# Gathers that add to turned products: an accumulating DMA, and clips on ScalarE, in a graph layer

## Chip, core and metric

One core of a Trainium2 chip runs the whole kernel. The metric is device time in microseconds: 4238.63 us, the median of three runs (4232.95 to 4239.72). All times of the profile are from one further execution of 4239.95 us, whose span (first to last instruction) is 4238.2 us.

## What is computed

A layer of a graph network on 12500 nodes with 96 features and 412500 edges, sorted by the target node. Cut to what matters:

```
_mlp(h, W, b, gamma, beta): h = relu(h @ W + b); normalize h over all rows (mean, variance); gamma * h + beta
node_feat = _mlp(x, W_node, ...)
edge_feat = _mlp(edge_attr, W_edge, ...)
message   = concatenate([x[row], x[col], edge_feat])      # row = src, col = dst
message   = _mlp(message, W_msg, ...)
agg       = segment_sum(message, col)
out       = layernorm(x + agg + node_feat)
```

So each edge's message is relu of a sum of three products: P[src], a row of the table P = x W_msg[0:96] of its source node; Q[dst], a row of the table Q of its target; and a product of the edge's own features.

## The kernel before

Edges stand in tiles of 128; four tiles make a group (512 edges, `GT` = 4, `GE` = 512), four groups a block (`BG` = 4). There are 3223 tiles, 806 groups and 202 blocks. A block's target nodes lie in a narrow window, so Q[dst] needs no gather: a matmul adds it from a window of Q's rows. P[src] does need one: `gather` (L205) issues, on POOL's queue, one indirect DMA per tile, which fetches 128 rows of 384 bytes into a tile `pg`. An index is given per partition.

The program has an opening and a loop. In the opening the tables P and Q are made and stored (`tables`), the edges' features are split and stacked (`split`, `places`), the node part is done (`nodes`) and the statistics of the edge features are taken (`edge_norm`), which the loop's weights `w_e` and `bias` need. POOL gathers meanwhile, in `blocks` (L220): rows of the first `SPILL` = 29 blocks go through a ring of `RING` = 14 groups (seven buffers of two) and are stored by SP to `spill` in HBM, two blocks behind (`BEHIND`). For the first `RAW` = 4 blocks the rows are those of x, since P is not there yet. Three tiles (`EARLY`) are fetched by SP in another way. At the end of the opening the same ring takes the rows of 14 groups more (L519).

`plan` makes the loop's order of blocks: the spilled ("early") ones are strewn among the other 173 ("late") ones. For a block at place s in that order the work is:

- SP: `load(s)` brings the edges' stacked features and the window of Q into `rhs`, three places ahead; `fetch` brings an early block's rows back into `pb`.
- PE and ScalarE: `edges` multiplies, `prepare` (L617) clips into `left`, two places ahead.
- PE and DVE: `linear` (L623) makes one group's product z, features by edges, in PSUM; `by_edge` (L632) turns it by three 32x32-wise transpositions into `zs`, edges by features, in SBUF. One place ahead, two buffers in the free end of `big`. One group's transpositions fill 32 partitions of all 16 tiles of the block.
- DVE: `message` (L639) takes two groups at once: h = clip(z + rows) by one custom instruction (`TENSOR_ADD_SAT`, L649), or a plain clip for raw blocks.
- ScalarE squares h (L663), DVE adds the squares up in PSUM (L674) and makes the matrix of places `at` (L655); PE adds h up by place (`sums`, L693), two groups behind; DVE adds the window to `agg` (L713).
- POOL: `ahead_of` (L489) gathers one group more for each late group taken in, 14 groups ahead.

The order on all engines in the loop is the one in which the program is written; each engine works its queue in order. A gather also waits for the gather eight before it, since eight semaphores go round.

## Time and profile before

| what | value |
|---|---|
| median of the runs | 4238.63 us |
| profiled execution, its span | 4239.95 us, 4238.2 us |
| gathers (from x, from P) | 64, 3156 |
| clipped adds on DVE with gathered rows, with spilled rows | 346, 50 |
| plain clips on DVE (raw blocks) | 8 |
| ScalarE, busy from 710 to 4176 us | 711.8 us |
| TensorE, busy from 710 to 4176 us, granted clock there | 2092.1 us, 0.79 |

The profile page gives, per engine, the time in which it was busy; a group of instructions has its count, its busy time and mean, and the idle time of the engine just before its instructions, with what ended it. "issue" is idle time in which nothing that the profile shows was waited for. PE is the matmul engine, PEld its weight loads, DVE the vector engine, ACT the scalar engine (ScalarE), POOL the engine that issues the gathers, SP the one that issues most other DMAs. A share of busy time over the whole span mixes opening, loop and tail; the views by window keep them apart.

### The profile page before, as it was taken

Reading aid. Unit: us, or ns where it says so; the run is one execution under the profiler, and the core shown is the slowest. Engines: PE = TensorE matmul, PEld = TensorE weight load, DVE = VectorE, ACT = ScalarE, POOL = GpSimd, SP = SyncE. Lnnn points to the kernel's source line nnn. Section 1 sums busy time; section 2 is a strip of 40 time slices with the busy share of each in tenths; the row PEclk is TensorE's granted clock in tenths of the full one; section 3 lists DMA queues with packets and bytes.
Section 4 is the critical chain, followed back from the end, with each engine's and each line's share of the span. In section 5 each row is a group of like instructions: output and inputs, shape, how many; then the busy total and the mean of one; then the engine's idle time right before and its main releaser. Section 6 shows DMA issues by size and latency. Waiting matters only on the chain.

```text
span 4238.2 us, 34504 instructions
## 1 busy us (share of the span) xinstructions
PE 2500.7 (59%) x10245; PEld 1391.0 (33%) x10245; DVE 3340.1 (79%) x4652; ACT 1117.9 (26%) x1229; POOL 3180.5 (75%) x3248
## 2 busy tenths in 40 slices
PE   4156664776655655666655565555655556666556
PEld 3041111433333332333333333333333333333335
DVE  2469998998887877878878887787878877878775
ACT  1438882222221211212112211111112112211111
POOL 7777776777777777777777777777777777777775
PEclk7557776888877787877777877787788787777776
DMA  8746562222222223222222222222222222222222
GB/s 229 267 139 149 134 148 51 57 57 64 50 56 53 57 71 78 63 56 56 55 56 50 57 54 55 57 57 54 56 57 53 50 63 50 54 57 55 56 44 64
DMA packets 215122, 316.63 MB, mean 75 GB/s; under 512 B 126785, under 2 KB 133275, under 8 KB 212095
## 3 DMA queue, kind: packets, MB, share of 16 engines
q0 software_dynamic: 103040, 158.48, 17.6%
q1 hardware_dynamic: 98923, 150.92, 12.1%
q10 hardware_dynamic: 12960, 4.93, 0.5%
q8 instruction: 82, 1.34, 0.1%
q14 instruction: 117, 0.96, 0.1%
HBM read 258.19 MB, written 55.89 MB: 74 GB/s over the span
## 4 chain that ended last, share of the span: by engine, by line
POOL 37%; DVE 25%; issue 19%; DMA 12%; PE 6%; ACT 1%; SPq 0%; DVEq 0%; POOLq 0%; ACTq 0%
POOL pg L210 37%; DMA pg<-p_tab,src 9%; DVE big L636 9%; DVE estats L419 8%; DVE h L649 3%; DVE mixed L674 2%; PE z L626 1%; PE pa L693 1%; PE py L981 1%; DVE at L655 1%; DMA q_tab<-trow 1%; PE py L383 1%; PE pt L194 0%; DMA x<-in_ea 0%; DVE part L424 0%
## 5 line engine op out<-in xcount | busy, mean ns | idle before, releaser
L210 POOL DMA_INDIRECT pg<-p_tab,src x3156 | 3097.6, 981 | 995.2 <-issue 899.6
L636 DVE STREAM_TRANSPOSE big<-z 32x512 f32<-32x512 f32 x2424 | 1715.3, 708 | 90.8 <-PE z L626 29.6
L693 PE MATMUL pa<-at,h 128*97 128x80 f32 x6446 | 934.1, 304 | 1346.3 <-DVE h L649 1327.5
L693 PEld LDWEIGHTS pa<-at,h 128*97 128x97 f32 x6446 | 881.7, 217 | 1818.7 <-DVE h L649 1677.1
L626 PE MATMUL z<-left,rhs 128*96 128x512 f32 (+1 forms) x1616 | 1079.7, 757 | 2.1 <-DVE big L636 2.1
L663 ACT ACTIVATE sq<-h 128x768 f32<-128x768 f32 x403 | 339.5, 842 | 2750.2 <-DVE h L649 2710.1
L649 DVE CUSTOM_DVE_ANT_0 h<-big,pg 128x768 f32<-128x768 f32 x346 | 325.3, 940 | 585.1 <-DMA pg<-p_tab,src 583.0
L621 ACT ACTIVATE left<-pr 127x1024 f32<-127x1024 f32 x404 | 405.6, 1004 | 18.1 <-PE pr L614 18.1
L674 DVE TENSOR_TENSOR mixed<-mixed,sq 128x768 f32<-128x768 f32 x401 | 387.7, 967 | 12.5
L419 DVE BATCH_NORM_STATS2 estats<-r 128x6 f32<-128x512 f32 x606 | 359.7, 682 | 11.8 <-ACT r L417 11.8
L417 ACT ACTIVATE r<-pr 128x1024 f32<-128x1024 f32 x303 | 309.0, 1025 | 102.2 <-PE pr L413 54.4
L413 PE MATMUL pr<-ea,wide 128*128 128x512 bf16 x606 | 237.8, 486 | 126.8 <-ACT r L417 116.7
L655 DVE TENSOR_TENSOR at<-rel,mixed 128x1264 f32<-128x1264 bf16 x202 | 296.5, 1468 | 6.8
L614 PE MATMUL pr<-late,we 128*128 128x512 bf16 x692 | 287.1, 507 | 23.4 <-DMA rhs<-q_tab 12.2
L626 PEld LDWEIGHTS z<-left,rhs 128*96 128x96 f32 x1616 | 264.1, 212 | 8.0 <-DVE big L636 6.5
L614 PEld LDWEIGHTS <-we 128*128 128x128 bf16 x808 | 103.3, 128 | 448.2 <-issue 446.5
L413 PEld LDWEIGHTS <-wide 128*128 128x128 bf16 x606 | 66.6, 110 | 297.4 <-issue 277.9
L383 PE MATMUL py<-center,big 96*128 96x96 f32 x196 | 42.8, 423 | 113.2 <-ACT big L378 100.2
L383 PEld LDWEIGHTS py<-center,big 96*128 96x128 f32 x196 | 42.0, 332 | 114.0 <-ACT big L378 100.6
L210 POOL DMA_INDIRECT pg<-in_x,src_raw x64 | 61.0, 952 | 20.9 <-issue 19.2
L194 PE MATMUL pt<-w_msg,big 96*128 96x192 f32 x196 | 37.8, 360 | 19.6 <-ACT trow L198 13.4
L200 DVE COPY trow<-pt 128x768 f32<-128x768 f32 x14 | 13.1, 956 | 44.5 <-DMA p_tab<-trow 20.7
(128 smaller groups left out, 696.6 us busy)
## 6 DMA issues: line engine op xcount, KB each, us to landing
pg<-p_tab,src POOLq DMA_INDIRECT x3156
pb<-spill SPq DMA_DIRECT2D x29, 768.0 KB
spill<-pg SPq DMA_DIRECT2D x55, 384.0 KB
ea<-stack_d SPq DMA_DIRECT2D x25, 480.0 KB
stack_d<-y SPq DMA_DIRECT2D x24, 448.0 KB
late<-stack_d SPq DMA_DIRECT2D x57, 180.0 KB
rhs<-q_tab SPq DMA_DIRECT2D x202, 46.5 KB
x<-in_ea SPq DMA_DIRECT2D x8, 896.0 KB
```

The source lines that it names most:

```text
L210: made = [nc.gpsimd.indirect_dma_start(out=pg[:, i, :], out_offset=None, in_=tab[:, :], in_offset=bass.IndirectOffsetOnAxis(ap=idx[:, i:i ...
L417: nc.scalar.activation(r, pr, AF.Relu)
L419: nc.vector.bn_stats(stats[:, (k - o) % NS, (k - o) // NS, :], r[:, 1 - o, :])
L614: nc.tensor.matmul(prs[s, half][:, i, :n], we[:, 2 * half + i, :], block[s][:, :n], start=True, stop=True)
L621: nc.scalar.activation(x[:C + WN, 2 * half:2 * half + 2, :n], pr[:C + WN, :, :n], AF.Relu)
L626: nc.tensor.matmul(zt[i % ZB][:C, :n], rhs[:KR, s % RB, i, :], left[s % 2][:KR, i, :n], start=True, stop=not raw)
L636: nc.vector.transpose(zs[s % 2][i * QE:(i + 1) * QE, :n // QE, q * QE:(q + 1) * QE], zt[i % ZB][q * QE:(q + 1) * QE, :n].rearrange("p (t e ...
L649: nc.vector._custom_dve(TENSOR_ADD_SAT, out=h, in0=z, in1=rows, s0=MOST, s1=0.0)
L655: nc.vector.tensor_tensor(at[s % AB][:, :m, :NW - 1], rel.rearrange("p g t -> p (g t)")[:, order[s] * BT:order[s] * BT + m].unsqueeze(2) . ...
L663: nc.scalar.activation(sq[:, :m, :n, :], hb[k // 2 % HP][:, k % 2:k % 2 + m, :n, :C], AF.Square)
L674: nc.vector.tensor_tensor(wide_sq, wide_sq, sq, op=OP.add)
L693: nc.tensor.matmul(by_place[s % 2][:C + 1, :NW], hb[k // 2 % HP][:r, k % 2, t, :], at[s % AB][:r, i * GT + t, :], start=i == 0 and t == 0, ...
```

## The change

- A late block's gathers no longer fill a buffer of their own. They are accumulating DMAs (`compute_op=OP.add`) whose target is the block's turned product in `zs`: each gathered row is added to the 96 numbers that stand there. So they come after the block's transpositions.
- `message` of late and raw blocks is then a clip at zero, on ScalarE (`AF.Relu`). Spilled blocks that aren't raw keep the clipped add on DVE.
- `zs` has six buffers, one block each: the four of the ring that the opening's plain gathers use, now whole blocks (16 groups instead of 14), and two in `big`.
- The loop turns block s+4 (`TURN`) while it takes in block s, and issues the gathers of block s+3 (`AFTER`); four blocks are turned ahead of the loop. Loads, `edges` and `prepare` are moved to as many places earlier (s+6, s+5).
- 32 blocks are spilled, 170 are late. `ahead_of` and the gathers at the opening's end are gone.

```diff
-SPILL = 29 * BG
-RING = 14
+SPILL = 32 * BG
+RING, MORE = 4, 2
+AFTER, TURN = 3, 4
...
-    ring = rpool.enter_context(tc.tile_pool(name="ring", bufs=RING // 2))
+    ring = rpool.enter_context(tc.tile_pool(name="ring", bufs=1))
+    ring = [ring.tile([P, BG, GT, C], F32, name=f"pg{i}") for i in range(RING)]
...
-    def gather(g, pg, without=0):
+    def gather(g, pg, without=0, plus=False):
...
-            in_offset=bass.IndirectOffsetOnAxis(ap=idx[:, i:i + 1], axis=0)).ins
+            in_offset=bass.IndirectOffsetOnAxis(ap=idx[:, i:i + 1], axis=0),
+            **(dict(compute_op=OP.add) if plus else {})).ins
...
-            for g in range(SPILL, SPILL + RING):
-                ahead_of(g)
...
-            zs = [big[:, NN - (i + 1) * BT * C:NN - i * BT * C].rearrange("p (t c) -> p t c", c=C) for i in range(2)]
+            zs = ring + [big[:, NN - (i + 1) * BT * C:NN - i * BT * C].rearrange("p (g t c) -> p g t c", t=GT, c=C)
+                         for i in range(MORE)]
...
-                if order[s] < RAW:
-                    nc.vector.tensor_scalar(h, z, 0.0, MOST, op0=OP.max, op1=OP.min)
-                    return
-                rows = got[g // 2 * 2].rearrange("p m t c -> p (m t) c")[:, o:o + n, :]
-                nc.vector._custom_dve(TENSOR_ADD_SAT, out=h, in0=z, in1=rows, s0=MOST, s1=0.0)
+                if RAW <= order[s] < SPILL // BG:
+                    rows = got[g // 2 * 2].rearrange("p m t c -> p (m t) c")[:, o:o + n, :]
+                    nc.vector._custom_dve(TENSOR_ADD_SAT, out=h, in0=z, in1=rows, s0=MOST, s1=0.0)
+                else:
+                    nc.scalar.activation(h, z, AF.Relu)
...
+                def turned(s, i):
+
+                    if s < len(order):
+                        linear(s, i)
+                        by_edge(s, i)
+
+                def rows_to(s, u):
+
+                    if s < len(order) and order[s] >= SPILL // BG and order[s] * BG + u < NG:
+                        gather(order[s] * BG + u, zs[s % len(zs)][:, u, :, :], plus=True)
...
+                for s in range(TURN):
+                    for i in range(BG):
+                        turned(s, i)
+                    if s < AFTER:
+                        for i in range(BG):
+                            rows_to(s, i)
...
-                    if s + 1 < len(order):
-                        linear(s + 1, u)
-                        by_edge(s + 1, u)
+                    turned(s + TURN, u)
+                    rows_to(s + AFTER, u)
...
-                    if g >= SPILL and ahead < SPILL + len(steps):
-                        ahead_of(ahead)
-                        ahead += 1
```

How this moves instructions is seen in the built programs' order. First POOL, from its first gather on: before (L210), all gathers but those of the raw blocks in two runs, with the load of `flag` between them, and then the sums of squares at the end.

```order
L210 DMA pg<-in_x,src_raw 128x96 x64
L210 DMA pg<-p_tab,src 128x96 x453
L719 TENSOR_LOAD flag
L210 DMA pg<-p_tab,src 128x96 x2703
L682 TENSOR_TENSOR sq<-sq 128x384
```

After (L212), around the load of `flag`; `pg_77` to `pg_80` are the four buffers of the ring, each holding a block of 16 tiles, and `big` stands for the two more.

```order
L212 DMA pg_79<-p_tab,src 128x96 x16
L212 DMA pg_80<-p_tab,src 128x96 x16
L715 TENSOR_LOAD flag
L212 DMA pg_77<-p_tab,src 128x96 x16
L212 DMA pg_78<-p_tab,src 128x96 x16
L212 DMA pg_79<-p_tab,src 128x96 x16
L212 DMA pg_80<-p_tab,src 128x96 x16
L212 DMA big<-p_tab,src 128x96 x32
```

Ahead of `flag` there are 509 gathers instead of 517, and behind it 2711 instead of 2703; those behind it write into buffers that DVE writes first.

Second DVE, at the loop's start: before, the last transpositions (L636) of block 0, with block 1's behind them and the first clipped adds (L649, shown as ISA) between; `z` are the two buffers in PSUM.

```order
L636 STREAM_TRANSPOSE big<-z_4966 32x16x32 x3
L636 STREAM_TRANSPOSE big<-z_4965 32x16x32 x3
L649 ISA h_4955<-big,pg 128x8x96
L636 STREAM_TRANSPOSE big<-z_4966 32x16x32 x3
L636 STREAM_TRANSPOSE big<-z_4965 32x16x32 x3
L649 ISA h_4956<-big,pg 128x8x96
L636 STREAM_TRANSPOSE big<-z_4966 32x16x32 x3
L674 TENSOR_TENSOR mixed<-mixed,sq 128x768
L655 TENSOR_TENSOR at_4962<-rel,mixed 128x16x79
```

After, from the end of the fourth block (its buffer is `pg_80`) on: the transpositions are L632, the squares' sum L670.

```order
L632 STREAM_TRANSPOSE pg_80<-z_4903 32x16x32 x3
L632 STREAM_TRANSPOSE big<-z_4902 32x16x32 x3
L632 STREAM_TRANSPOSE big<-z_4903 32x16x32 x3
L632 STREAM_TRANSPOSE big<-z_4902 32x16x32 x3
L632 STREAM_TRANSPOSE big<-z_4903 32x16x32 x3
L670 TENSOR_TENSOR mixed<-mixed,sq 128x768
L651 TENSOR_TENSOR at_4899<-rel,mixed 128x16x79
L632 STREAM_TRANSPOSE big<-z_4902 32x16x32 x3
```

Four blocks are turned ahead of the loop and a fifth in its first step, and no clipped add stands among them; the clips are on ScalarE, each just ahead of its square.

Third SP, whose queue opens the loop: before, the last stores of spilled rows (L237), the first loads of features (`late`), twelve rows of `bias` (L538) that complete `rhs`, and the windows of Q (L578).

```order
L237 DMA spill<-pg 128x768 x4
L719 TENSOR_LOAD flag
L360 DMA late_4967<-stack_d 32x1536
L360 DMA late_4967<-stack_d 16x1536
L538 DMA rhs<-bias 1x16x6 x12
L360 DMA late_4967<-stack_d 60x1536
```

After, the same place (L240, L533):

```order
L240 DMA spill<-pg_79 128x768 x2
L240 DMA spill<-pg_80 128x768
L715 TENSOR_LOAD flag
L363 DMA late_4904<-stack_d 32x1536
L363 DMA late_4904<-stack_d 16x1536
L533 DMA rhs<-bias 1x16x6
L240 DMA spill<-pg_80 128x768
L533 DMA rhs<-bias 1x16x6 x11
```

The last store, of the second half of block 31, which waits for the last plain gathers, now stands behind the first of the bias rows.

More of the change, by code (lines that the diff above doesn't have):

```diff
@@ L225, in blocks @@
                 for i in range(0, BG, 2):
-                    pg = ring.tile([P, 2, GT, C], F32, name="pg")
+                    pg = ring[b % RING][:, i:i + 2, :, :]
                     for k in range(2):
@@ L487, in fast @@
         y0s, got = [], {}
-        def ahead_of(g):
-            if g % 2 == 0:
-                got[g] = ring.tile([P, 2, GT, C], F32, name="pg")
-            if g < NG:
-                gather(g, got[g // 2 * 2][:, g % 2, :, :])
         with tc.manual_schedule(engines={ET.SP, ET.Pool}):
@@ L632, in by_edge @@
             def by_edge(s, i):
-                n = columns(s)
+                n, z = columns(s), zs[s % len(zs)].rearrange("p g t c -> p (g t) c")
                 for q in range(C // QE):
-                    nc.vector.transpose(zs[s % 2][i * QE:(i + 1) * QE, :n // QE, q * QE:(q + 1) * QE],
+                    nc.vector.transpose(z[i * QE:(i + 1) * QE, :n // QE, q * QE:(q + 1) * QE],
                                         zt[i % ZB][q * QE:(q + 1) * QE, :n].rearrange("p (t e) -> p t e", e=QE))
@@ L642, in message @@
                 o = k % 2 * GT
-                z = zs[s % 2][:, g % BG * GT:g % BG * GT + n, :]
+                z = zs[s % len(zs)].rearrange("p g t c -> p (g t) c")[:, g % BG * GT:g % BG * GT + n, :]
                 h = hb[k // 2 % HP].rearrange("p m t c -> p (m t) c")[:, o:o + n, :C]
-                if order[s] < RAW:
-                    nc.vector.tensor_scalar(h, z, 0.0, MOST, op0=OP.max, op1=OP.min)
-                    return
-                rows = got[g // 2 * 2].rearrange("p m t c -> p (m t) c")[:, o:o + n, :]
-                nc.vector._custom_dve(TENSOR_ADD_SAT, out=h, in0=z, in1=rows, s0=MOST, s1=0.0)
+                if RAW <= order[s] < SPILL // BG:
[3 more added lines that the diff above has]
+                    nc.scalar.activation(h, z, AF.Relu)
             def places_of(s):
@@ L715, in fast, with first @@
             loads = list(range(-(-NB // NBY)))
-            n, ahead = len(steps), SPILL + RING
+            n = len(steps)
             with tc.manual_schedule(engines={ET.SP, ET.Pool, ET.PE, ET.DVE, ET.Activation}):
                 bad = nc.values_load(flag, min_val=0, max_val=1, skip_runtime_bounds_check_because="a comparison's result")
+                def turned(s, i):
[5 more added lines that the diff above has]
+                        gather(order[s] * BG + u, zs[s % len(zs)][:, u, :, :], plus=True)
+                def first(s, half):
+                    if s < len(order):
+                        edges(s, half)
+                        prepare(s, half)
                 for s in range(3):
@@ L723, in fast @@
                     for half in range(2):
-                        edges(s, half)
-                        prepare(s, half)
+                        first(s, half)
                 places_of(0)
-                for i in range(BG):
-                    linear(0, i)
-                    by_edge(0, i)
+                for s in range(TURN):
[4 more added lines that the diff above has]
+                            rows_to(s, i)
+                    if s + 3 < TURN + 2:
+                        load(s + 3)
+                    if s + 2 < TURN + 1:
+                        for half in range(2):
+                            first(s + 2, half)
+                assert min(order.index(b) for b in range(RAW)) >= TURN + 2
                 waiting, last = None, BG * (len(order) - 1)
@@ L734, in fast @@
                     if u == 0:
-                        if s + 3 < len(order):
-                            load(s + 3)
-                        if s + 2 < len(order):
-                            fetch(s + 2)
+                        if s + TURN + 2 < len(order):
+                            load(s + TURN + 2)
+                        for o in (TURN + 2, 2):
+                            if s + o < len(order) and (order[s + o] < RAW) == (o > 2):
+                                fetch(s + o)
                     if k >= LATER:
@@ L755, in fast @@
                         add(j // BG, place(j // BG))
-                    if s + 2 < len(order):
+                    o = s + TURN + 1
+                    if o < len(order):
                         if u % 2 == 0:
-                            edges(s + 2, u // 2)
+                            edges(o, u // 2)
                         else:
-                            prepare(s + 2, u // 2)
-                        if u == 3 and order[s + 2] < RAW:
-                            transposed(s + 2)
-                    if g >= SPILL and ahead < SPILL + len(steps):
-                        ahead_of(ahead)
-                        ahead += 1
+                            prepare(o, u // 2)
+                        if u == 3 and order[o] < RAW:
+                            transposed(o)
                     if k >= 200 and k % 4 == 0 and loads:
```

## Prediction

> **What bounds the kernel now.** I read the page's busy times first, then the groups of POOL, then who waits for whom. The first rows are the page's busy line and its groups that matter here (line, engine, operation, shapes, count, busy time, mean of one in ns, then the idle time before them).

> ```profile
> span 4238.2 us, 34504 instructions
> ...
> PE 2500.7 (59%) x10245; PEld 1391.0 (33%) x10245; DVE 3340.1 (79%) x4652; ACT 1117.9 (26%) x1229; POOL 3180.5 (75%) x3248
> ...
> L210 POOL DMA_INDIRECT pg<-p_tab,src x3156 | 3097.6, 981 | 995.2 <-issue 899.6
> L636 DVE STREAM_TRANSPOSE big<-z 32x512 f32<-32x512 f32 x2424 | 1715.3, 708 | 90.8 <-PE z L626 29.6
> ...
> L649 DVE CUSTOM_DVE_ANT_0 h<-big,pg 128x768 f32<-128x768 f32 x346 | 325.3, 940 | 585.1 <-DMA pg<-p_tab,src 583.0
> ...
> L210 POOL DMA_INDIRECT pg<-in_x,src_raw x64 | 61.0, 952 | 20.9 <-issue 19.2
> ```

> DVE has the longest busy time, but it is not the bound: it idles 583.0 us because gathered rows have not landed. POOL's gathers take 3097.6 us and their "issue" gaps 899.6 us more, together nearly the whole span of 4238.2 us. The waits of POOL from 640 us on say the same (waiter, what it waited for, total, times, longest):

> ```profile
> POOL pg L210 <- issue: 780.0, 2558, 0.3
> POOL pg L210 <- DMA pg<-p_tab,src: 41.2, 135, 0.3
> POOL pg L210 <- DVE h L649: 18.1, 1, 18.1
> POOL pg L210 <- DVE big L636: 7.9, 26, 0.3
> ```

> Apart from one stop of 18.1 us, no gap is longer than 0.3 us, which is what every gather has before it. So the end is set by **when POOL may start its last run of gathers, how many there are, and what each one takes**. The rest is the tail behind the last one.

> What one takes is not constant. Grouped over 400 to 600 us (before the loop) and over 760 to 4100 us (in the loop):

> ```profile
> L210 POOL DMA_INDIRECT pg<-p_tab,src x158 | 149.4, 946 | 51.2 <-issue 45.7 <-DMA spill<-pg 4.5 <-DMA erow<-p_tab 0.9
> ...
> L210 POOL DMA_INDIRECT pg<-p_tab,src x2605 | 2546.0, 977 | 794.3 <-issue 740.0 <-DMA pg<-p_tab,src 39.3 <-DVE big L636 7.6
> ...
> L649 DVE CUSTOM_DVE_ANT_0 h<-big,pg 128x768 f32<-128x768 f32 x329 | 310.2, 943 | 558.7 <-DMA pg<-p_tab,src 556.7
> ...
> L649 DVE CUSTOM_DVE_ANT_0 h<-big,pb 128x768 f32<-128x768 f32 x50 | 46.5, 931 | 0.3
> ```

> In the loop a gather means 977 ns and 305 ns of gap (794.3 / 2605); before the loop 946 ns. The 31 ns more are 2605 x 0.031 = 80.8 us. The timeline shows where they fall:

> ```profile
> 1515.28 0.95 POOL L210 DMA_INDIRECT pg<-p_tab,src  x1 [0.30 <-issue]
> 1516.53 1.25 POOL L210 DMA_INDIRECT pg<-p_tab,src  x1 [0.30 <-DMA pg<-p_tab,src]
> 1518.08 0.94 POOL L210 DMA_INDIRECT pg<-p_tab,src  x1 [0.30 <-issue]
> ...
> 1516.05 0.91 DVE L649 CUSTOM_DVE_ANT_0 h<-big,pg 128x768 f32<-128x768 f32 x1
> ```

> The long gather, 1.25 us, begins while DVE's clipped add is running, and its neighbours beside transposes take 0.94 to 0.95. I charge the 80.8 us to the 379 clipped adds of that window (329 and 50): **0.213 us each**. An undisturbed gather then has a slot of 0.946 + 0.305 = **1.251 us**.

> [...]

> **The change part by part.** Here are the loop's opening and end in the timeline:

> ```profile
> 691.44 0.94 POOL L210 DMA_INDIRECT pg<-p_tab,src  x1 [0.30 <-issue]
> 710.50 0.95 POOL L210 DMA_INDIRECT pg<-p_tab,src  x1 [18.12 <-DVE h L649]
> ...
> 698.48 10.90 DVE L636 STREAM_TRANSPOSE big<-z 32x512 f32<-32x512 f32 x15 [9.30 <-PE z L626]
> ...
> 632.13 2.56 SPq L237 DMA_DIRECT2D spill<-pg  x4
> 678.21 7.56 SPq L538 DMA_DIRECT2D rhs<-bias  x12
> ...
> 4175.19 0.95 POOL L210 DMA_INDIRECT pg<-p_tab,src  x1 [0.30 <-issue]
> ```

> The busy times by window (PE, PEld, DVE, ACT, POOL, each with its count; granted clock, DMA share, GB/s) count POOL's run:

> ```profile
> 710.00:4176.00 3466.00, 2092.13 (x8948) 1185.02 (x8948) 2781.70 (x3815) 711.80 (x811) 2641.66 (x2703) 0.79 0.24 56
> ```

> *Counts.* 3220 gathers before and after (3156 + 64). Before, 2703 are behind the stop and 517 ahead of it. After, the plain ones are 32 x 16 - 3 = 509, and 2711 accumulate: eight more behind the stop, 8 x 1.251 = **+10.0 us**.

> *The start.* A transposition writes 32 partitions of all 16 tiles of a block, a gather adds to 128 partitions of one tile: the first accumulating gather needs all twelve transpositions of its block. At 10.90 / 15 = 0.727 us each, from 698.48, they end at 707.2. I add the usual 0.3 us gap and 0.6 us, since on SP's queue one store of spilled rows (2.56 / 4) now stands among the bias rows that everything here waits for: **708.1 us**, 2.4 us ahead of the 710.50 of now, which waited for a first clipped add to free a buffer. That store waits for the last plain gather, number 509; now that one starts at 691.44 - 8 x 1.25 = 681.4, so at worst SP stands still about 5 us there. The ring of plain gathers is 16 groups instead of 14, which lets POOL run ahead by a half block (10 us) more and so, I take it, not be late. Bounds of the start: 707.5 to 713.

> *The rate.* 396 clipped adds (346 + 50) become 56, two for each of 28 spilled blocks. 340 x 0.213 = **-72.4 us**. ScalarE takes the rest:

> ```profile
> L663 ACT ACTIVATE sq<-h 128x768 f32<-128x768 f32 x403 | 339.5, 842 | 2750.2 <-DVE h L649 2710.1
> ...
> L674 DVE TENSOR_TENSOR mixed<-mixed,sq 128x768 f32<-128x768 f32 x401 | 387.7, 967 | 12.5
> ...
> L655 DVE TENSOR_TENSOR at<-rel,mixed 128x1264 f32<-128x1264 bf16 x202 | 296.5, 1468 | 6.8
> ```

> A clip of this size is not in the trace on ScalarE; by the square of the same size, 842 ns, 348 clips are 293 us on an engine that waits 2710.1 us for exactly these messages. They are hidden, and DVE loses 340 x 0.94 us of work, which is worth nothing since DVE was waiting. Behind a clip that waits for rows stand on ScalarE the square and the next `left`; `left` is made five blocks ahead, so nobody waits for it soon. The three more spilled blocks (six stores, three loads) ride on SP beside POOL's run.

> *The new wait.* Each block's first gather waits for DVE. The loop turns block s+4 while it takes in block s, so when POOL is at the block that is being taken in, three whole blocks, at least two of them with gathers to do, are turned: 2 x 16 x 1.251 = 40 us of cover. DVE's own work for a block is 12 x 0.708 of transposing, 2 x 0.967 of squares and 1.468 of places, 11.9 us and some small adds, against 20 us of POOL. I cost this wait at nothing; if the cover were gone, each microsecond per block would cost 170 us.

> *The gather itself.* The trace holds no accumulating gather. [...] I take **946 ns**, the row it is nearest to: the same 128 rows, the same indices, the same bytes out of the table. [...]

> *The sum.* 708.1 + 2711 x 1.251 + 56 x 0.213 = 708.1 + 3391.5 + 11.9 = 4111.5 us for the end of the last slot. The same sum for the kernel now, 710.5 + 2703 x 1.251 + 396 x 0.213, gives 4176.3; the trace has 4175.19 + 1.25 = 4176.4. The tail is 4238.2 - 4176.4 = 61.8 us, and I add 1 us for the clip and for a landing that adds: span 4174.3. The profiled execution lasted 1.75 us more than its span (4239.95), so 4176 against 4239.95; the runs shown have a median 1.3 us lower (4238.63), hence **4175 us**, 1.5% less.

> **The rivals.**

> *B, the other side: POOL works longer on a gather that adds.* Place: each of the 2711 gathers. [...] Price: 27.1 us for every 10 ns; it decides from (4238.6 - 4175) / 2711 = 23.5 ns, only 2.5% of 946. At half as much again (473 ns) the time is 4175 + 1282 = 5457, at double 6740.

> [...]

> *C: the 16 DMA engines become the bound.*

> ```profile
> q0 software_dynamic: 103040, 158.48, 17.6%
> ```

> 17.6% of 16 engines over 4238.2 us, by 3220 gathers, is 0.23 us on each engine for its eight rows. The limit is the slot of 1.251 us, or 156 ns per row. Plain rows leave a factor of 5.4; if each adding row took what eight take now, 0.23 us, a gather would hold an engine 1.85 us, and POOL, which waits for the gather eight before, would go at that rate: 4175 + 2711 x 0.60 = 5800. Against it: twice the bytes alone are 0.46 us.

> *D: the long gathers stay long,* because something else than the clipped add stretches them (rows landing, for instance, which is when a clipped add starts). Then 72.4 us are not saved: 4247, no change.

> **How the numbers follow.** A, the forecast: 0.52, with a range of its own from 4150 to 4225 (the slot to 5 ns, 14 us; start, tail and remaining adds to 10 us; upward also a gather up to 15 ns dearer). B: 0.27. C: 0.12. D: 0.09. A measurement tells about 0.2%, or 8.5 us, from no change. Faster: A and a bit of C or D below 4230, 0.53; same: D, 0.08; slower: B and C, 0.39. A alone is 0.52, so the range must reach into B: up to 5460 it takes in A, D and B to half as much again; left out are B's far part (0.10), most of C (0.08) and 0.01 below. So 4150 to 5460.

> **What would show it.** Right: the group of gathers in the loop near 950 ns with gaps of 0.305; POOL's waits without an entry for DVE or DMA above 0.3 us, save one stop that ends near 708; 56 clipped adds; the last gather near 4110. B shows in the mean of that group, C in long waits of POOL for its own earlier gathers and a share of their queue many times 17.6%, D in a mean still near 977. If turned blocks come too late, POOL's waits name DVE's transposition with gaps far over 0.3 us. I am wrong above all if an adding gather costs POOL 24 ns more than a plain one.

## The result and the profile after

| | before | after |
|---|---|---|
| median of the runs | 4238.47 us | 5847.15 us |
| lowest to highest, 4 runs each | 4232.95 to 4239.72 | 5846.11 to 5847.83 |
| ratio after to before, 95% interval | | 1.3799 [1.3775, 1.3823] |
| span of the profiled execution | 4238.2 us | 5844.3 us |

The forecast was 4175 us, its range 4150 to 5460. The kernel is 38% slower, above the range.

The first rows are the page of the changed kernel: engines, the queue of the gathers, the share of each engine in the chain that ended last, and its groups of gathers and of clips.

```profile
span 5844.3 us, 34880 instructions
...
PE 2657.9 (45%) x10099; PEld 1521.5 (26%) x10245; DVE 3038.1 (52%) x4304; ACT 1410.5 (24%) x1577; POOL 4783.6 (82%) x3248
...
q0 software_dynamic: 406672, 158.48, 24.9%
...
POOL 71%; issue 16%; DVE 7%; DMA 3%; PE 2%; ACT 1%; SPq 0%; another core or an unknown queue 0%; POOLq 0%; ACTq 0%; DVEq 0%
...
L645 ACT ACTIVATE h<-pg 128x768 f32<-128x768 f32 x216 | 181.2, 839 | 2153.2 <-DMA pg<-p_tab,src 2153.0
...
L645 ACT ACTIVATE h<-big 128x768 f32<-128x768 f32 x132 | 111.2, 842 | 1592.2 <-DMA big<-p_tab,src 1592.2
```

POOL went from 3180.5 to 4783.6 us of work, 1603 us more, and the span grew by 1606 us. The other engines wait for it: ScalarE's clips, the new consumers, stand 2153.0 + 1592.2 us for rows. Bytes of the gathers' queue are the same 158.48 MB as before. The groups of POOL from 1000 to 5500 us, where every gather adds, show where the work is:

```profile
L212 POOL DMA_INDIRECT pg<-p_tab,src x1440 | 2280.6, 1584 | 438.6 <-issue 436.5 <-DMA pg<-p_tab,src 1.2 <-DVE at L651 0.3
L212 POOL DMA_INDIRECT big<-p_tab,src x961 | 1489.8, 1550 | 292.7 <-issue 291.4 <-DMA big<-p_tab,src 1.2
```

Two of the six blocks in the ring (`big`) show the undisturbed value, **1550 ns** against 946 before; the gap is still 0.305 us (292.7 / 961). The other four (`pg`) have 34 ns more on the mean. The timeline shows the first gather that adds, and two that meet a clipped add of a spilled block:

```profile
704.08 1.59 POOL L212 DMA_INDIRECT pg<-p_tab,src  x1 [36.16 <-DVE pg L632]
...
1483.19 2.59 POOL L212 DMA_INDIRECT pg<-p_tab,src  x1 [0.30 <-issue]
1483.45 0.90 DVE L643 CUSTOM_DVE_ANT_0 h<-pg,pb 128x768 f32<-128x768 f32 x1
...
1486.09 1.55 POOL L212 DMA_INDIRECT pg<-p_tab,src  x1 [0.30 <-issue]
...
1489.74 0.96 DVE L643 CUSTOM_DVE_ANT_0 h<-pg,pb 128x768 f32<-128x768 f32 x1
1489.80 2.32 POOL L212 DMA_INDIRECT pg<-p_tab,src  x1 [0.30 <-issue]
```

The loop's run starts at 704.1 us. A clipped add stretches a gather by 1.04 and 0.77 us here. Over all 56 adds the gathers that overlap one took 50.1 us more than 1.550 each, **0.89 us per add**, and the other 2655 show no excess (0.3 ns in the mean). Rebuilt from these terms, 704.1 + 2711 x (1.550 + 0.305) + 50.1 = 5783 us; the last gather ends at 5782.4, and 61.9 us of tail follow.

How far a clipped add stretches a gather can be read off these rows. The gather takes its 1.55 us and, on top, the time from its own start to the add's end, less 0.12 us. The add at 1489.74 ends 0.90 us behind the gather's start, and the gather takes 1.55 + 0.90 - 0.12 = 2.33 us (2.32 in its row); the other ends 1.16 us behind it, and 1.55 + 1.16 - 0.12 = 2.59. So the price of an add isn't a constant: it depends on where in a gather the add falls.

In three of the five series of runs behind this one the kernel before itself took 5540 to 5551 us instead of 4237 to 4243, for a reason that the traces don't name (in e1_plain's, taken there, DVE stands still for up to 31.0 us at a time), so that of those series only ratios within a series, durations of single gathers (a plain one takes 943 ns in both kinds of series, e1 and e1b below) and lengths of POOL's own run where it has no stop are used.

### The profile page after: what moved, and what is told of

It reads as the page before. It is cut to its first block, busy times and chain, and to the rows that moved or that the text cites. A ratio compares the mean times of both kernels' runs of the same rounds, so it can differ in the third digit from the quotient of the medians.

```text
span 5844.3 us, 34880 instructions
## 1 busy us (share of the span) xinstructions
PE 2657.9 (45%) x10099; PEld 1521.5 (26%) x10245; DVE 3038.1 (52%) x4304; ACT 1410.5 (24%) x1577; POOL 4783.6 (82%) x3248
## 3 DMA queue, kind: packets, MB, share of 16 engines
q0 software_dynamic: 406672, 158.48, 24.9%
## 4 chain that ended last, share of the span: by engine, by line
POOL 71%; issue 16%; DVE 7%; DMA 3%; PE 2%; ACT 1%; SPq 0%; another core or an unknown queue 0%; POOLq 0%; ACTq 0%; DVEq 0%
POOL pg L212 44%; POOL big L212 27%; DVE estats L422 5%; PE py L1000 1%; PE py L386 0%; DMA x<-in_ea 0%; DMA pg<-p_tab,src 0%; DMA p_tab<-trow 0%; DMA big<-p_tab,src 0%; PE pt L196 0%; DVE nstats L374 0%; DVE big L380 0%; DMA q_tab<-trow 0%; PE z L622 0%; PE pa L689 0%
## 5 line engine op out<-in xcount | busy, mean ns | idle before, releaser
L212 POOL DMA_INDIRECT pg<-p_tab,src x2100 | 3064.1, 1459 | 676.7 <-issue 633.3
L632 DVE STREAM_TRANSPOSE pg<-z 32x512 f32<-32x512 f32 x1632 | 1155.0, 708 | 2232.9 <-PE z L622 2156.0
L689 PE MATMUL pa<-at,h 128*97 128x80 f32 x6446 | 1024.4, 325 | 2739.3 <-ACT h L645 2614.6
L212 POOL DMA_INDIRECT big<-p_tab,src x1056 | 1637.1, 1550 | 321.6 <-issue 319.2
L689 PEld LDWEIGHTS pa<-at,h 128*97 128x97 f32 x6446 | 978.8, 238 | 3186.7 <-ACT h L645 2891.4
L622 PE MATMUL z<-left,rhs 128*96 128x512 f32 (+1 forms) x1616 | 1168.6, 815 | 44.0 <-DVE big L632 33.3
L645 ACT ACTIVATE h<-pg 128x768 f32<-128x768 f32 x216 | 181.2, 839 | 2153.2 <-DMA pg<-p_tab,src 2153.0
L632 DVE STREAM_TRANSPOSE big<-z 32x512 f32<-32x512 f32 x792 | 562.0, 710 | 259.0 <-PE z L622 245.8
L645 ACT ACTIVATE h<-big 128x768 f32<-128x768 f32 x132 | 111.2, 842 | 1592.2 <-DMA big<-p_tab,src 1592.2
L670 DVE TENSOR_TENSOR mixed<-mixed,sq 128x768 f32<-128x768 f32 x401 | 387.5, 966 | 85.5 <-ACT sq L659 73.1
L622 PEld LDWEIGHTS z<-left,rhs 128*96 128x96 f32 x1616 | 285.6, 227 | 67.9 <-DVE big L632 38.9
L212 POOL DMA_INDIRECT pg<-in_x,src_raw x64 | 60.7, 948 | 20.8 <-issue 19.2
## 6 DMA issues: line engine op xcount, KB each, us to landing
rhs<-q_tab SPq DMA_DIRECT2D x202, 46.5 KB
```

Source lines behind the costliest of these rows:

```text
L212: made = [nc.gpsimd.indirect_dma_start(out=pg[:, i, :], out_offset=None, in_=tab[:, :], in_offset=bass.IndirectOffsetOnAxis(ap=idx[:, i:i ...
L622: nc.tensor.matmul(zt[i % ZB][:C, :n], rhs[:KR, s % RB, i, :], left[s % 2][:KR, i, :n], start=True, stop=not raw)
L632: nc.vector.transpose(z[i * QE:(i + 1) * QE, :n // QE, q * QE:(q + 1) * QE], zt[i % ZB][q * QE:(q + 1) * QE, :n].rearrange("p (t e) -> p t ...
L670: nc.vector.tensor_tensor(wide_sq, wide_sq, sq, op=OP.add)
L689: nc.tensor.matmul(by_place[s % 2][:C + 1, :NW], hb[k // 2 % HP][:r, k % 2, t, :], at[s % AB][:r, i * GT + t, :], start=i == 0 and t == 0, ...
```

## The experiments

The theories: **M**, POOL works longer on a gather that adds. **S**, the new order and its waits cost the time. For what stays of the forecast: **V**, a clipped add stretches the gathers beside it because two of its operands lie in SBUF; **D**, something else stretches them. Most of these kernels leave a part of the messages out, or add old rows to them, as their texts say, and serve for their times alone; e9, e12 and e13 compute everything.

**Is it the add?** In e1_plain one argument goes, so that the same 2711 gathers overwrite z:

```
-            **(dict(compute_op=OP.add) if plus else {})).ins
+            **{}).ins
```

> The changed kernel with its 2711 accumulating gathers made plain (they overwrite z, so z is left out of these messages). Everything else stays: order, waits, the clip on ScalarE, 56 clipped adds, 32 spilled blocks. Theory M (the add itself makes POOL's work longer): a gather goes back to 946 ns, the time to 5847 - 2711 x 0.604 = about 4210 us. Rival S (the new order and its waits cost the time, whatever the gather does): near 5850 us. Clipped adds: 0.21 us each by the trace of before, 0.89 by that of after (12 or 50 us in all).

It took 5512.94 us where the kernel before took 5549.74. The same kernel in another series, e1b:

> The same kernel as e1_plain once more (accumulating gathers made plain, z left out of these messages): where e1_plain ran, the kernel before took 5549.74 us instead of 4238.47, so its time says nothing. Theory M (the add makes POOL's work longer): gather 946 ns, time 5847 - 2711 x 0.604 = 4210 us with 56 clipped adds at 0.89 us, 4175 with them at 0.21. Rival S (the new order and its waits cost the time): near 5850 us.

Measured: 4184.9 us, kernel before 4243.25, ratio 0.9864 [0.9848, 0.9881]. In its profiled execution (4176.29 us, the fastest of four) the gathers from 760 to 4100 us are

```profile
L212 POOL DMA_INDIRECT pg<-p_tab,src x1601 | 1535.1, 959 | 487.9 <-issue 461.7 <-DMA pg<-p_tab,src 17.4 <-ACT sq L659 5.8
L212 POOL DMA_INDIRECT big<-p_tab,src x1056 | 996.3, 943 | 321.8 <-issue 307.8 <-DMA big<-p_tab,src 11.9 <-PE z L622 0.9
```

943 ns where no clipped add falls, as plain gathers take, and no wait of POOL on DVE over 0.3 us after the first one. S is out: order, turned blocks ahead, clip on ScalarE and spilled blocks are all still in this kernel, which is 1.4% faster than the one before. Its first plain gather in place of an adding one starts at 704.6, and its 56 clipped adds cost 24.5 us, 0.44 each. It gains 58 us on its kernel before; with the forecast's 0.213 for each add it would be 12.6 us more, 71, against 64 forecast.

**The add alone in the kernel before.** e2b lets the ring's gathers add to what their buffers hold, in fixed buffers:

```
+    ring = [ring.tile([P, 2, GT, C], F32, name=f"pg{i}") for i in range(RING // 2)]
...
-                gather(g, got[g // 2 * 2][:, g % 2, :, :])
+                gather(g, got[g // 2 * 2][:, g % 2, :, :], plus=True)
```

> The kernel before with one thing alone of the change: the gathers behind the spilled blocks add to what their buffer holds (so old rows are summed into the messages), in fixed buffers of the same size. Theory M: 1550 ns per gather; 2703 of them and the rest of the sum of before give 710.5 + 2703 x 1.8545 + 62 = 5785 us, and 396 clipped adds on top: 5870 us with 0.21 us each as in before, 6139 us with 0.89 us each as in the changed kernel. Rival S: near 4240 us.

6850.47 us, over both values (kernel before 4243.25): with fixed buffers the first group of a pair was issued ahead of the message that frees its buffer, so that each message waited for rows fourteen groups on, and POOL for the message (1098.6 us in 337 waits). The total is that of my edit's own wait; its gathers took 1556 ns. e2c issues both groups of a pair behind the message:

```
-                    if g >= SPILL and ahead < SPILL + len(steps):
-                        ahead_of(ahead)
-                        ahead += 1
+                    if g >= SPILL and u % 2:
+                        for _ in range(2):
+                            if ahead < SPILL + len(steps):
...
```

> As e2b_before_adding (the kernel before, its ring's gathers add to what the buffer holds, so old rows are summed into the messages), with the two groups of a pair gathered together behind the message that frees their buffer. In e2b the first group of a pair was issued ahead of that message, so each message waited for rows fourteen groups on. Theory M: 1550 ns per gather and no stop of POOL for VectorE; 710.5 + 2703 x 1.8545 + 62 = 5785 us and the 396 clipped adds on top: 5870 us at 0.21 us each, 6139 us at 0.89 us each (the price that the 56 adds of the changed kernel have).

It took 6188.85 us (kernel before 5540.12), but POOL's run has no stop from 918.5 us on. From 1000 to 6000 us its gathers, clipped adds beside them and all, are

```profile
L211 POOL DMA_INDIRECT pg<-p_tab,src x2604 | 4207.0, 1616 | 794.3 <-issue 790.9 <-DMA pg<-p_tab,src 2.7 <-DVE big L638 0.6
```

The last 2711 run from 918.5 to 6125.0 us with gaps of 0.305. That is 5206.5 us, 1.92 per gather, so the add alone gives the long gathers in the old order as well (M); those that overlap no clipped add take 1550 ns. Less 2711 x 1.8545 = 5027.5 there are 179 us over, 0.45 for each of the 396 clipped adds: between the two prices expected.

**What in it costs: rows, bytes, or the instruction?** Gathers of 64 rows, plain (e4) and adding (e3), and adding ones of half rows (e5b). In e4 and e3 the list of indices is cut to 64 in the same way (not shown), and e4 drops the add besides:

```
-            out=pg[:, i, :], out_offset=None, in_=tab[:, :],
+            out=pg[:64 if plus else P, i, :], out_offset=None, in_=tab[:, :],
...
```

In e5b:

```
-            out=pg[:, i, :], out_offset=None, in_=tab[:, :],
+            out=pg[:, i, :C // 2 if plus else C], out_offset=None,
+            in_=tab.rearrange("n (h c) -> (n h) c", h=2) if plus else tab[:, :],
...
```

The indices stay as they were on a table that is now read in half rows, so by the edit these are other half rows than the first halves that its text names; their number and size are as it says. The "last run" in the first text is the one of the second.

> As the last run, with plain gathers of 64 rows (partitions 0 to 63; the other half of the rows is left out). Theory R (a fixed part and a part per row that is read: a + 128 b = 946, a + 256 b = 1550, so b = 4.72 ns, a = 342 ns): 644 ns per gather. If all of it goes by the row: 473 ns; if all is fixed: 946 ns. The time is then no longer set by POOL alone.

> The changed kernel with accumulating gathers of 64 rows only (the other half of the rows is left out). Theory R (each row that is read costs the same, an adding row is read twice): 342 + 128 x 4.72 = 946 ns, the time near 4210 us. Rival F (a fixed surcharge for an instruction that adds): that of the plain gather of 64 rows + 604 ns, 1248 ns if that one is 644, the time near 5030 us. All by the row, nothing fixed: 775 ns.

> The changed kernel with accumulating gathers of 128 rows of 48 numbers instead of 96 (the second half of every row is left out). Theory R (the cost goes by rows, not by bytes): 1550 ns and 5847 us as in the changed kernel, with half the bytes. Rival Y (the surplus of 604 ns is for bytes that are read twice): 946 + 302 = 1248 ns or less, near 5030 us.

They took 5756.73, 5675.63 and 6066.69 us, one run each, where the kernel before took 5549.74. The gathers themselves, from 1000 to 5300 us, in that order, one fence for each kernel:

```profile
L212 POOL DMA_INDIRECT big<-p_tab,src x979 | 885.7, 905 | 746.8 <-issue 708.2 <-DVE big L632 25.2 <-DMA big<-p_tab,src 13.4
```

```profile
L212 POOL DMA_INDIRECT big<-p_tab,src x992 | 1410.0, 1421 | 302.2 <-issue 299.4 <-DMA big<-p_tab,src 1.8 <-PE pa L689 0.6
```

```profile
L212 POOL DMA_INDIRECT big<-p_tab,src x928 | 1437.9, 1549 | 283.1 <-issue 281.9 <-DMA big<-p_tab,src 0.6 <-PE z L623 0.6
```

Half the bytes: 1549 ns, no change, so bytes cost POOL nothing here (rival Y is out). Half the rows: 905 ns plain and 1421 adding. "Every row that is read costs the same" (R: 644 and 946) is out by far, and F (plain + 604, 1509 with this plain one) is near: the surcharge falls only from 604 to 516 ns. Four sizes in one kernel (e11; the list of indices is cut alike), adding in every second group:

```
-            out=pg[:, i, :], out_offset=None, in_=tab[:, :],
+            out=pg[:P - 32 * i if plus else P, i, :], out_offset=None, in_=tab[:, :],
...
-            **(dict(compute_op=OP.add) if plus else {})).ins
+            **(dict(compute_op=OP.add) if plus and g % 2 else {})).ins
```

> The changed kernel with the four gathers of each group cut to 128, 96, 64 and 32 rows (the other rows are left out), adding in every second group and plain in the others: eight durations in one trace. Theory F' (from the runs of 64 and 128 rows: adding 1292 + 2.0 ns per row, plain 854 + 0.72 ns per row): adding 1550, 1486, 1421, 1357 ns; plain 946, 923, 900, 877 ns. Theory R (two reads per row at 4.72 ns, 342 fixed): adding 1550, 1248, 946, 644; plain 946, 795, 644, 493. If a gather of under 128 rows takes another path: steps instead of a line.

Eight rows of its timeline, adding ones of 128, 96, 64 and 32 rows, then plain ones:

```profile
3001.84 1.59 POOL L212 DMA_INDIRECT big<-p_tab,src  x1 [0.30 <-issue]
3003.73 1.46 POOL L212 DMA_INDIRECT big<-p_tab,src  x1 [0.30 <-issue]
3005.50 1.42 POOL L212 DMA_INDIRECT big<-p_tab,src  x1 [0.30 <-issue]
3007.23 1.34 POOL L212 DMA_INDIRECT big<-p_tab,src  x1 [0.30 <-issue]
3008.87 1.01 POOL L212 DMA_INDIRECT big<-p_tab,src  x1 [0.30 <-issue]
3010.19 0.95 POOL L212 DMA_INDIRECT big<-p_tab,src  x1 [0.30 <-issue]
3011.45 0.92 POOL L212 DMA_INDIRECT big<-p_tab,src  x1 [0.30 <-DMA big<-p_tab,src]
3012.67 0.88 POOL L212 DMA_INDIRECT big<-p_tab,src  x1 [0.30 <-issue]
```

Close to F' (1.55, 1.49, 1.42, 1.36 and 0.95, 0.92, 0.90, 0.88), and far from R. Over the whole run the means of the sizes below 128, without the gathers beside a clipped add, are 1464, 1424 and 1340 ns adding and 951, 916 and 875 plain, each within 28 ns of F', with no step below 128 rows. At 32 rows the surcharge is still 0.46 us, at 128 it is 0.60 (1550 - 946, from the changed kernel and the one before): through these two, about **0.42 us for the instruction and 1.4 ns for each row**, an estimate that meets 64 rows and lies 0.04 us over 96. What POOL does in the 0.42 us the traces don't show. The first gather behind a change of kind takes 0.04 to 0.07 us more (1.59 and 1.01), and in this kernel that is each one of 128 rows; so does the first adding one of the changed kernel (1.59 at 704.08). The total was 4856.48 us.

**What a clipped add costs.** e7 takes the 56 clipped adds out of the changed kernel (the spilled blocks' rows are left out):

```
-                if RAW <= order[s] < SPILL // BG:
+                if False:
```

> The changed kernel without its 56 clipped adds (the spilled blocks' rows are left out, their products are clipped on ScalarE as the others). Theory V, with the price read from the changed kernel's trace (0.89 us for each add beside an adding gather): no gather over 1.57 us in the loop, 5847 - 50 = 5797 us. With 0.21 us each: 5835 us. If long gathers have another cause: 5847 us.

It took 6018.93 us, the kernel before 5550.55. From 1000 to 5500 us:

```profile
L212 POOL DMA_INDIRECT pg<-p_tab,src x1463 | 2267.0, 1550 | 446.3 <-issue 439.9 <-DVE agg L709 2.4 <-DMA pg<-p_tab,src 2.4
L212 POOL DMA_INDIRECT big<-p_tab,src x965 | 1495.2, 1549 | 294.4 <-issue 292.0 <-DMA big<-p_tab,src 1.8 <-DMA pg<-p_tab,src 0.3
```

`pg` is down from 1584 to 1550. From the start of its first adding gather (922.4) to the end of the last one (5950.1) POOL takes 5027.7 us; in the changed kernel it is 5782.4 - 704.1 = 5078.3. The 56 adds cost 50.7 us, 0.9 each, as read from the trace, and no gather of e7's run is over 1.59 us.

In e6, made from the kernel before, ScalarE clips the gathered rows alone, and DVE has no clipped add:

```
-                nc.vector._custom_dve(TENSOR_ADD_SAT, out=h, in0=z, in1=rows, s0=MOST, s1=0.0)
+                nc.scalar.activation(h, rows, AF.Relu)
```

> The kernel before with its 396 clipped adds on VectorE replaced by a clip of the gathered rows on ScalarE (z is left out of the messages). Theory V (the clipped add, with two operands in SBUF, stretches gathers beside it by 0.213 us each): every gather at 946 ns, 4238 - 84 = 4154 us. Rival D (long gathers come from landing rows or something else): 977 ns in the mean as before, 4238 us.

Measured 4143.27 us, kernel before 4243.25, ratio 0.9765 [0.9749, 0.9782]. From 760 to 4050 us:

```profile
L210 POOL DMA_INDIRECT pg<-p_tab,src x2630 | 2488.2, 946 | 801.9 <-issue 763.5 <-DMA pg<-p_tab,src 35.1 <-ACT left L621 1.2
```

The long gathers are gone but for four of 2700 (977 to 946 in the mean): D is out. Between the profiled spans 97.4 us are saved (4238.2 to 4140.8): POOL's run behind the stop is 83.9 us shorter, as V has it, and it begins 13.5 us earlier, at 697.0, chiefly because the stop at the loop's start, which waited for a first clipped add, shrank from 18.1 to 6.5 us. The four that stay long (1.10 to 1.30 us) each lie beside one of the eight plain clips of the raw blocks, which have one operand in SBUF: a clipped add isn't the only instruction of DVE that does this.

That two operands in SBUF are enough, and that it needn't be this custom instruction, the kernel before shows by itself. Of its gathers behind 711 us that begin while a clipped add is running (with more than 0.16 us of it left), 245 take 1216 ns in the mean. Those that begin so under the sum of squares (L674) or the matrix of places (L655), which have one operand in PSUM, take 946 in the mean, 396 and 201 of them. And in its opening a plain subtraction of two tensors in SBUF (L316) does what the clipped add does:

```profile
105.22 2.03 DVE L316 TENSOR_TENSOR x<-x,y 128x1792 f32<-128x1792 f32 x1 [7.09 <-ACT y L315]
105.58 2.48 POOL L210 DMA_INDIRECT pg<-p_tab,src  x1 [0.30 <-issue]
```

The subtraction ends 1.67 us behind the gather's start, and 0.946 + 1.67 - 0.12 = 2.50.

**Can the two gains be had with the whole computation?** e9 is the kernel before with `SPILL = 30 * BG`, one more block; e12 copies each group's rows into a PSUM bank on ScalarE, so that the clipped add has one operand in SBUF; e13 does both.

```
-SPILL = 29 * BG
+SPILL = 30 * BG
...
-                nc.vector._custom_dve(TENSOR_ADD_SAT, out=h, in0=z, in1=rows, s0=MOST, s1=0.0)
+                r = rp[:, :n * C].rearrange("p (t c) -> p t c", c=C)
+                nc.scalar.activation(r, rows, AF.Copy)
+                nc.vector._custom_dve(TENSOR_ADD_SAT, out=h, in0=z, in1=r, s0=MOST, s1=0.0)
...
-                    if u % 2:
-                        message(k - 1)
+                    message(k, 1, GT)
```

> The kernel before with 30 spilled blocks instead of 29 and nothing else. Theory: POOL's stop of 18.1 us at the loop's start is filled with the 16 gathers (20 us) of one more block: 4243 - 18 = 4225 us. Rival: the stop is moved (the ring's first clipped add is waited for all the same, or the block's store and load cost as much): 4243 us.

> The kernel before, whole computation, with the gathered rows of each group copied by ScalarE into a PSUM bank, from which VectorE's clipped add (128x384, twice as many) takes them: one operand in SBUF instead of two. The two accumulators of the sums by place share one bank for that. Theory V (two operands in SBUF are what stretches gathers): gathers back to 946 ns in the mean, 4243 - 84 = 4159 us. Rival D: 977 ns, 4243 us. Rival W (ScalarE's copy and VectorE's add wait for one another over the single bank, and VectorE falls behind the gathers): over 4243 us, with POOL waiting for VectorE.

> e12_rows_in_psum with 30 spilled blocks (whole computation). If both theories hold: 4159 - 18 = 4141 us, 2.4% less than the kernel before. If only the first: 4159; if only the second: 4225; if VectorE falls behind: over 4243 us.

In two series where the kernel before took 5540.12 and 5550.55 us their ratios to it were 0.9958, 1.0595 and 1.0624 for e9, e12 and e13, then 0.9895, 1.0618 and 1.056:

> e9_spill30 once more (the kernel before with 30 spilled blocks, whole computation): 4225 us if the stop at the loop's start is filled, 4243 if it is only moved.

> e12_rows_in_psum once more (whole computation): where it ran, the kernel before took 5540.12 us, with VectorE standing still for up to 17 us at a time, so its time says little; all its gathers took 943 ns, as theory V says. Where the kernel before takes its 4240 us: theory V 4243 - 84 = 4159 us; rival W (ScalarE's copy and VectorE's add wait for one another) over 4243 us, with stops of POOL named after the copy.

> e13_psum_spill30 once more (whole computation, 30 spilled blocks), for the same reason. Both theories: 4159 - 18 = 4141 us; only the operand in PSUM: 4159; only the 18 us stop: 4225.

Two of them where the kernel before took 4236.68 us:

> e9_spill30 a third time (the kernel before with 30 spilled blocks, whole computation). Where the kernel before takes 4240 us: 4225 us if the stop is filled, 4243 if it is moved. On a chip of the other kind: 0.4 to 1% faster than the kernel before, as twice so far.

> e13_psum_spill30 a third time (whole computation; rows copied into PSUM, 30 spilled blocks); both runs so far fell on chips where the kernel before takes over 5500 us. Where it takes 4240 us: theory V and the filled stop 4159 - 18 = 4141 us; rival W (copy and add wait for one another over the single bank) over 4240 us. On a chip of the other kind: again about 6% slower than the kernel before.

e9c: **4221.33 us**, kernel before 4236.68, ratio 0.9962 [0.9949, 0.9976]. The stop is filled: its gathers run through from 633 us to the last one at 4160.0, with no gap over 0.32 us. Of the 18.1 us the time gives 15.4; this version is 0.4% faster than the kernel before. e13c: 4317.42 us, ratio 1.0193 [1.0179, 1.0207], 1.9% slower. Its gathers and adds from 760 to 4200 us, and then its waits of POOL:

```profile
L210 POOL DMA_INDIRECT pg<-p_tab,src x2623 | 2475.3, 944 | 965.3 <-issue 743.6 <-ACT rp L652 177.5 <-DMA pg<-p_tab,src 36.3
...
L653 DVE CUSTOM_DVE_ANT_0 h<-big,rp 128x384 f32<-128x384 f32 x758 | 418.4, 552 | 31.3 <-ACT rp L652 13.6
...
L652 ACT ACTIVATE rp<-pg 128x384 f32<-128x384 f32 x655 | 321.0, 490 | 806.0 <-DVE h L653 806.0
```

```profile
POOL pg L210 <- ACT rp L652: 177.8, 39, 9.1
```

With one operand in PSUM the clipped adds stretch no gather (944 ns), which is V once more, now with z in the sum. But each copy waits for the add ahead of it to leave the bank, POOL waits 177.8 us for the copies to free the ring, and that is rival W. By an estimate the span of 4315.4 would be 4137.6 without these waits, near the 4141 expected; it leaves the stretch behind the last gather at its 84 us, against 62 in the kernel before. Whether two banks or another place for the copy reach that was not tried.

## Why the prediction was wrong

*The gather itself: the step that failed.* "I take 946 ns, the row it is nearest to" was the wrong choice: an accumulating gather takes 1550 ns. That it moves the same rows, indices and bytes was no reason to take 946: POOL's cost hardly goes with rows (0.6 ns each of a plain gather, (946 - 905) / 64) and, for one that adds, not with bytes at all (1549 ns at half of them, e5b). 2711 x 0.604 = 1637 us. The text named this the point on which it would be wrong, with a break-even of 23.5 ns, and had half as much again to double in rival B; the measured 64% lies between. But it gave B 0.27 and stopped the range at half as much again, although no row spoke for 946 beyond likeness.

*The clipped adds.* 0.213 us each was right as a mean for before, and so was the clipped add as the cause (without it gathers take 946 ns in e6 and 1549 to 1550 in e7); V, its two operands in SBUF, agrees with e13c (944 ns with one of them in PSUM). As a price to carry over it was too small: 0.44 beside plain gathers in e1b, 0.45 and 0.89 beside adding ones in e2c and the changed kernel. Here that is 56 x (0.894 - 0.213) = 38 us. The traces show why a mean doesn't carry over: a gather is stretched by the time from its start to the add's end, less 0.12 us, so a new order of the same instructions has a new price. In before 138 of the 396 adds stretch nothing, in the changed kernel 5 of 56.

*The start.* 708.1 forecast, 704.1 measured, 4 us early; in its bounds of 707.5 to 713 it wasn't. The opening itself was that much shorter: the first of the bias rows on SP's queue starts at 674.29 instead of 678.21 (why stays open), and the store behind it took 0.51 us of the 0.6 charged.

Together: 4175 + 1637 + 38 - 4 = 5846 against 5847 measured. *Counts, tail and cover were right:* 2711 gathers behind the stop, 61.9 us of tail (62.8 forecast), ScalarE's clip at 839 to 842 ns (842 taken) and hidden, and no wait of POOL on DVE over 0.3 us after the one at the start. What the forecast is worth without the dearer gather e1b shows: 58 us gained instead of 64.

*Rivals.* B happened. Its upper price, double, no run shows: the measured gather takes 1.64 times the plain one. A cost that doubles per row isn't the whole of it either: by rows of this case it would leave a 32-row gather with a quarter of the 0.604 us, and it keeps 0.46. C is out: POOL waits 0.3 us at most for its own DMAs, and the queue holds 24.9% of the engines' span, although it moves 406672 packets instead of 103040. Nor does POOL's instruction seem to wait inside for the engines to take its rows: with half the rows, and 15.1% of the engines' span, it still takes 1421 ns. D is out by e6 and e7: the clipped add costs gathers 0.21 to 0.89 us each time in the mean, and nothing with one operand in PSUM (944 ns, e13c), and the plain subtraction of two SBUF tensors at L316 stretches them in the same way (2.48 us for 0.95). Which part of a gather they hold up, no run here shows.

## What to carry to other kernels

Where one engine issues thousands of like instructions and sets the end, a change to the instruction itself must be priced by a run or left wide open: here 24 ns of 946 decided, and the add cost 604. Here the accumulating gathers took 302 us of busy time from DVE (3340.1 to 3038.1) that was not missed, and gave POOL 1603 us more (3180.5 to 4783.6). Whether that pays off where the vector engine is the bound, no run here shows. The stop in the bounding engine's row at the loop's start was the cheap gain: one more spilled block fills it, for 0.4%.
